# Cross attention on one core: a tile's probabilities turned in 32x32 blocks by VectorE and sent through DRAM, in place of sixteen TensorE transposes

## The chip, the core and the metric

The kernel runs on one core of a Trainium2 chip. The metric is the time of one execution on the device in microseconds (us). TensorE (PE) does the matmuls and the transposes, VectorE (DVE) and ScalarE (ACT) read the PSUM banks and do elementwise work, GpSimd (POOL) does elementwise work on SBUF, and SyncE (SP) issues every DMA, in program order. Each engine's order is the order in which the program is written.

## The reference

An encoder layer over 2 x 77 context rows, then a decoder layer over 2 x 2048 rows of width 512: causal self-attention, cross attention on the 77 encoded rows, and a feed-forward part of width 2048. All of it is float32. The part that matters here is the cross attention (16 heads of width 32, 77 keys):

```python
def _mha(xq, xkv, w_in, b_in, w_out, b_out, bias):
    ...
    scores = jnp.einsum('bhqd,bhkd->bhqk', q, k) / jnp.sqrt(jnp.asarray(hd, xq.dtype))
    scores = scores + bias[None]
    attn = jax.nn.softmax(scores, axis=-1)
    out = jnp.einsum('bhqk,bhkd->bhqd', attn, v)
    out = out.transpose(0, 2, 1, 3).reshape(Bq, Tq, D)
    return out @ w_out.T + b_out
...
y = y + _mha(yn, yn, dec_sa_in_w, dec_sa_in_b, dec_sa_out_w, dec_sa_out_b, sb)
y = y + _mha(_ln(y, dec_n2_s, dec_n2_b), memory, dec_ca_in_w, dec_ca_in_b, dec_ca_out_w, dec_ca_out_b, cb)
h = _ln(y, dec_n3_s, dec_n3_b)
y = y + (jax.nn.relu(h @ dec_ff1_w.T + dec_ff1_b) @ dec_ff2_w.T + dec_ff2_b)
```

## The kernel before

The 4096 decoder rows are eight blocks of 512 rows, each of four tiles of 128 rows. The first part of the program is the encoder and the self-attention, with the cross attention of block 0 (`first_cross`) strewn into it. The second part (TensorE's first product of it stands at 1632 us) is the feed-forward part of the eight blocks; the cross attention of block x+1 (`cross`) is laid between the products of block x.

The feed-forward part of a block has 56 slots (`ff_slot`). In slots 0 to 27 (`first_product`) a slot uses one weight tile of 256 KB; in slots 28 to 55 (`second_product`) four slots use 2, 2, 2 and 1 tiles, each with four matmuls of 128 columns (L1665). `feed` (L1539) reloads the ring `w_ring` of 16 such tiles at the end of each slot: it issues as many loads as tiles were used, each into the place of a tile that the slot has just finished, so SP waits for that slot's matmuls. In slots 28 to 31 `new_y` (L1359) also loads a 256 KB tile of the rows of the block after next, as long as there is one.

`cross` fills a table `plan` of 56 entries; before each `ff_slot` the stages of that slot's entry are written. A tile's attention (`attend_stages`) has the stages `score` (L822, then the bias, maxima and differences on VectorE), `exp` (ScalarE, L835), `sums` (VectorE, L840), `normalize` (GpSimd, L846), `turned`, and `times_v` (L860). `turned` makes 16 TensorE transposes of 128 x 77 into PSUM (L852) and four ScalarE copies to `pts` (L853), one buffer that the four tiles use in turn. Tile t has its stages at slots 13 + 5t plus 0, 2, 3, 3, 7 and 11. The products with the output weights (`o_product`, L1799) stand in slots 31 to 34 for tiles 0 and 1 and in 40 to 43 for tiles 2 and 3; the last normalization of the four tiles (`norm_stages`: statistics, centring, TensorE transposes L797) begins at slots 35, 36, 44 and 45.

PSUM has eight banks; in this part `bank()` hands out four in turn for the cross attention, and the feed-forward products hold the other four.

Of the kernel before, what the change touches and what calls it, by code (L numbers as in the profile page):

```python
# [10 lines left out]
F32 = mybir.dt.float32  # L11
AF = mybir.ActivationFunctionType
# [5 lines left out]
P = 128  # L18
B, T, S, D = 2, 2048, 77, 512
H, HD, DFF = 16, 32, 2048  # L20
# [3 lines left out]
MB = 512  # L24
# [30 lines left out]
def tile_encoder_decoder(ctx: ExitStack, tc: tile.TileContext, ins, out):  # L55
# [103 lines left out]
    with (  # L159
# [30 lines left out]
        def rows4(r):  # L190
            return slice(r * HD, (r + 1) * HD)
# [618 lines left out]
        def attend_stages(q, kTc, v, y, biased, pr, pts, place, w_o, bi=None):  # L810


            prh = pr.rearrange("p (h k) -> p h k", k=S)
            by_r = pr.rearrange("p (g r k) -> p g r k", r=HC, k=S)
            keep = {}

            def score():
                mx = sm.tile([P, NC, HC], F32, name="cmx", tag="cmx", bufs=3)
                banks = [bank() for _ in range(HC)]
                for g in range(NC):  # L820
                    for r in range(HC):
                        nc.tensor.matmul(  # L822
                            banks[r][:, ts(g, S)], q(g)[rows4(r)], kTc[rows4(r), g, :], start=True, stop=True
                        )
# [12 lines left out]
            def sums():  # L837
                su = sm.tile([P, H], F32, name="csu", tag="csu", bufs=2)
                ri = sm.tile([P, H], F32, name="cri", tag="cri", bufs=2)
                nc.vector.tensor_reduce(su, prh, AX.X, ALU.add)  # L840
                nc.vector.reciprocal(ri, su)
                keep["ri"] = ri

            def normalize():
                ri = keep["ri"]
                nc.gpsimd.tensor_tensor(prh, prh, ri[:, :, None].to_broadcast([P, H, S]), ALU.mult)  # L846

            def turned():
                for g in range(NC):
                    pt = bank()  # L850
                    for r in range(HC):
                        nc.tensor.transpose(pt[:S, ts(r, P)], prh[:, g * HC + r, :], ident)  # L852
                    nc.scalar.copy(pts(g), pt[:S, :])  # L853

            def times_v():
                ot = bank()
                for g in range(NC):
                    for r in range(HC):
                        h = g * HC + r
                        nc.tensor.matmul(  # L860
                            ot[rows4(r), ts(g, P)], v[:, ts(h, HD)], pts(g)[:, ts(r, P)], start=True, stop=True
                        )
                keep["oT"], keep["bank"] = place(), ot
                nc.scalar.copy(keep["oT"], ot)

            def out():
                mm, oT = bank(), keep["oT"]
                for c in range(NC):
                    nc.tensor.matmul(mm, oT[:, ts(c, P)], w_o[:, c, :], start=(c == 0), stop=(c == NC - 1))
                nc.vector.tensor_tensor(y(), mm, y(), ALU.add)  # L870

            return score, exp, sums, normalize, turned, times_v, out, keep

        def first_cross():
# [21 lines left out]
            def pts(g):  # L896
                return kT[:S, g, 2 * MB : 3 * MB]

            def loads():
                for t in range(TB):  # L900
# [667 lines left out]
        mixed = oflat[:, H * S : H * S + 12 * P].rearrange("p (k n) -> p k n", n=P)  # L1568
        lefts = {}

        def by_f(tile):
# [153 lines left out]
        def cross(x):  # L1725
# [79 lines left out]
            for n, js in Q_SLOTS.items():  # L1805
                plan[n].append(lambda js=js: [q_product(j) for j in js])
            for n, js in O_SLOTS.items():
                t = 0 if n < 36 else 2
                plan[n].append(lambda t=t, js=js: [o_product(t, j) for j in js])
            bias_1 = None  # L1810
            if m == 0:

                def next_batch():
                    nc.sync.dma_start(kTc, ckT_d[:, :, ts(b, S)])
                    nc.sync.dma_start(vc[0][:S, :], cv_d[:, b, :])

                plan[1].append(next_batch)

                spare = [y_of(x + 1, r) for r in range(HC)]
                bias_1 = [a[:, : NC * S].rearrange("p (g k) -> p g k", k=S) for a in spare]  # L1820
                plan[3].append(lambda: bias_tile(prs[0].rearrange("p (h k) -> p h k", k=S), 2, P, S, 255))
                plan[5].append(lambda: [bias_tile(a, 2, P, S, 255 - P, r, HC) for r, a in enumerate(bias_1)])
            for t in range(TB):
                at = 13 + 5 * t
                y = lambda t=t: y_of(x, t)
                biased = m == 0 and t < 2
                fs = attend_stages(
                    lambda g, t=t: qT[g // 2][:, g % 2, ts(t, P)], kTc, vc[0][:S, :], y, biased, prs[t % 2],
                    lambda g: pts_all[:S, g, :], place("xr"), wbt,
                    bias_1 if biased and t else None,  # L1830
                )
                held["o", t] = fs[7]
                if t % 2:
                    fs = fs[:5] + (lambda t=t, f=fs[5]: [f(), sums_o(t - 1)],)
# [4 lines left out]
                at = (35, 36, 44, 45)[t]  # L1839
                for k, f in zip((0, 2, 4), fs):  # L1840
                    plan[at + k].append(f)
                rows_later[x * per + 15 + t] = fs[3]
            for fs in plan:
                for f in fs:
# [84 lines left out]
        for n in range(end):  # L1929
# [21 lines left out]
            for step in script_of(n):  # L1951
                if step in ("a", "d"):
                    k = to_turn.pop(0)
                    turn([(n, k, r) for r in range(HC)], step)
                    turned.append(k)
                    assert len(turned) <= pts_all.shape[1]
                    leave(n, k)
                elif step == "E":
                    exps(1)
                elif step == "J":  # L1960
                    while parts:
                        parts.pop(0)()
                elif step == "j":
                    parts.pop(0)()
                elif step == "S" and may_score() and stream[0][0] <= n + 2:
                    two = stream[0][1] == 0 and may_score(1) and stream[1][0] == stream[0][0]
                    score_next(1 if two else 0)
                elif step in ("v", "V"):
                    values(n, turned, not to_turn, step == "V")
                    turned = []  # L1970
                elif step == "F":
                    feed(turned_to[n])
# [69 lines left out]
```

## Time and profile before

| | |
|---|---|
| median of 3 runs | 2705.1 us (2704.49 to 2707.9) |
| the profiled execution's own time | 2708.39 us |
| its span | 2706.3 us, mean granted TensorE clock 0.998 |
| TensorE, weight loads, VectorE, ScalarE, GpSimd busy | 99%, 81%, 68%, 56%, 37% |
| DMA | 385.10 MB, 142 GB/s over the span; 153 to 241 GB/s in the slices of the second part |

A profiled execution is about 3 us above the median. The rows of the trace name a line of the kernel, the engine, the operation, the tiles written and read, and the duration. TensorE's ends are modelled, so how long a group of matmuls holds it is read from where the next group starts.

### The profile page before, as it was taken

The numbers are of one execution on the slowest core, as the hardware profiler recorded it, in microseconds if no ns is written. First come the engines' busy times: TensorE is split into PE (matmuls) and PEld (weight loads), VectorE is DVE, ScalarE is ACT, GpSimd is POOL, SyncE is SP. The second block draws the span as 40 slices with busy tenths as digits, with TensorE's granted clock in tenths as the row PEclk, the third lists the DMA queues.
The fourth block names the chain that finished last, engine by engine and source line by source line (L and its number), as shares of the span: only waits on it lengthen the run. The fifth ranks groups of instructions, "written<-read, shape, count | busy, mean of one in ns | idle before, by whom it ended". The sixth has DMA issues, their size and how long they took to land.

```text
span 2706.3 us, 68257 instructions
## 1 busy us (share of the span) xinstructions
PE 2684.3 (99%) x26606; PEld 2199.2 (81%) x26606; DVE 1848.9 (68%) x5448; ACT 1526.2 (56%) x2960; POOL 1002.3 (37%) x844
## 2 busy tenths in 40 slices
PE   9999999999999999999999999999999999999998
PEld 6678777777776677778777887999999898989898
DVE  4776688888885687788888883737464746464635
ACT  3545567767886557777767794444443444444431
POOL 2602235500300513223300103556565555556546
PEclk9999999999999999999999999999999999999999
DMA  8734445511213522343311216565658565657575
GB/s 235 215 99 131 128 146 174 169 59 43 64 49 87 144 80 81 111 126 118 107 53 40 73 59 196 176 211 172 215 169 241 172 215 171 215 170 216 153 222 186
DMA packets 296276, 385.10 MB, mean 142 GB/s; under 512 B 41184, under 2 KB 165648, under 8 KB 295826
## 3 DMA queue, kind: packets, MB, share of 16 engines
q1 hardware_dynamic: 295954, 380.73, 46.9%
q8 instruction: 211, 3.46, 0.5%
q14 instruction: 111, 0.91, 0.1%
HBM read 334.15 MB, written 46.47 MB: 141 GB/s over the span
## 4 chain that ended last, share of the span: by engine, by line
PE 96%; DVE 1%; ACT 1%; DMA 1%; POOL 1%; SPq 0%; issue 0%; DVEq 0%; POOLq 0%; ACTq 0%
PE psum L417 18%; PE psum L1636 15%; PE psum L1665 13%; PE psum L375 11%; PE psum L441 9%; PE psum L1120 8%; PE psum L1799 3%; PE psum L1756 3%; PE psum L1035 3%; PE psum L852 2%; PE psum L822 1%; PE psum L860 1%; PE psum L576 1%; PE psum L797 1%; PE psum L239 1%; PE psum L215 1%
## 5 line engine op out<-in xcount | busy, mean ns | idle before, releaser
L406 ACT ACTIVATE pp<-pp,nm 128x128 f32<-128x128 f32 (+15 forms) x512 | 611.4, 1200 | 23.4 <-DVE nm L401 23.2
L384 DVE TENSOR_SCALAR_CACHE_REDUCE pp<-psum 128x512 f32<-128x512 f32 (+3 forms) x1024 | 556.7, 590 | 69.2 <-PE psum L375 67.1
L423 ACT COPY pts<-psum 128x512 f32<-128x512 f32 x696 | 374.4, 593 | 346.3 <-PE psum L417 309.5
L417 PE MATMUL psum<-ident,pp 128*128 128x128 f32 x4352 | 527.4, 276 | 5.7 <-ACT nT L310 4.0
L417 PEld LDWEIGHTS psum<-ident,pp 128*128 128x128 f32 x4352 | 475.2, 141 | 64.5 <-issue 21.4
L441 PEld LDWEIGHTS psum<-pts,vv 128*32 128x32 f32 x8704 | 225.7, 110 | 119.4 <-DVE pp L384 49.3
L375 PE MATMUL psum<-kT,q 32*128 32x512 f32 (+3 forms) x2560 | 320.3, 565 | 2.2 <-ACT kT L231 1.4
L421 DVE COPY pts<-psum 128x512 f32<-128x512 f32 x392 | 257.7, 686 | 84.8 <-PE psum L417 81.3
L1665 PE MATMUL psum<-pp 128*128 128x128 f32 x2560 | 304.5, 276 | 1.9 <-POOL pp L948 1.6
L1665 PEld LDWEIGHTS psum<-pp 128*128 128x128 f32 x2560 | 296.3, 192 | 8.6 <-issue 2.8
L441 PE MATMUL psum<-pts,vv 128*32 128x128 f32 x8704 | 278.0, 275 | 1.1 <-DVE pp L384 0.8
L948 POOL TENSOR_TENSOR pp<-pp 128x512 f32<-128x512 f32 x159 | 212.8, 1355 | 110.2 <-ACT pp L800 45.4
L1636 PE MATMUL psum<-vv,pp 128*128 128x256 f32 x1024 | 236.2, 381 | 0.0
L1636 PEld LDWEIGHTS psum<-vv,pp 128*128 128x128 f32 x1024 | 190.3, 190 | 25.8 <-issue 0.5
L391 DVE CUSTOM_DVE_ANT_0 pp<-psum,bias 128x256 f32<-128x256 f32 (+1 forms) x512 | 196.0, 411 | 13.2 <-PE psum L375 12.7
L375 PEld LDWEIGHTS psum<-kT,q 32*128 32x128 f32 x2560 | 127.5, 183 | 87.3 <-issue 50.0
L1649 DVE TENSOR_TENSOR kT<-kT,psum 128x512 f32<-128x512 f32 x96 | 65.8, 686 | 191.1 <-PE psum L1636 190.9
L1652 ACT ACTIVATE kT<-kT,vecs 128x256 f32<-128x256 f32 x192 | 86.9, 501 | 156.6 <-DVE kT L1649 155.9
L1636 PE MATMUL psum<-nT,pp 128*128 128x256 f32 x768 | 174.1, 380 | 0.0
L1636 PEld LDWEIGHTS psum<-nT,pp 128*128 128x128 f32 x768 | 144.2, 190 | 20.3 <-issue 1.6
L1673 ACT COPY oT<-psum 128x128 f32<-128x128 f32 x56 | 15.0, 268 | 239.1 <-PE psum L1665 239.1
L480 POOL TENSOR_TENSOR oT<-rirows,oT 128x512 f32<-128x512 f32 x30 | 38.4, 1279 | 288.6 <-DMA rirows<-rec 267.0
(272 smaller groups left out, 4108.2 us busy)
## 6 DMA issues: line engine op xcount, KB each, us to landing
pp<-w_d SPq DMA_DIRECT2D x520, 256.0 KB
pp<-in_dec_ff_wT_dram SPq DMA_DIRECT2D x112, 256.0 KB
bias<-tzg SPq DMA_DIRECT2D x128, 128.0 KB
pp<-wo_d SPq DMA_DIRECT2D x56, 256.0 KB
wqk<-in_dec_sa_in_wT_dram SPq DMA_DIRECT2D x52, 256.0 KB
wqk<-sa_q SPq DMA_DIRECT2D x84, 128.0 KB
vv<-in_enc_ff_wT_dram SPq DMA_DIRECT2D x8, 1024.0 KB
xr<-in_x_dram SPq DMA_DIRECT2D x32, 256.0 KB
```

Of the source, the lines that this page charges most:

```text
L375: nc.tensor.matmul(banks[r][:, : kn * P], q[rows4(r), ts(t, P)], kT[rows4(r), g, k0 * P : (k0 + kn) * P], start=True, stop=True,)
L384: nc.vector.tensor_scalar(p[:, k0 : k0 + far], s[:, :far], 1.0, None, ALU.mult, ALU.max, accum_out=st["mx"][:, r, c : c + 1],)
L391: nc.vector.tensor_tensor_reduce(p[:, k0 + far : i + 1], s[:, far:kn], near[:, 2 - (kn - far) :], 1.0, LOWEST, ALU.add, ALU.max, accum_out ...
L406: nc.scalar.activation(p, p, AF.Exp, bias=nm, accum_out=to)
L417: nc.tensor.transpose(pt[:, ts(x, P)], state[n]["p"][r][:, k], ident)
L421: nc.vector.tensor_copy(pts[:, : len(load), :], pt[:, :w])
L423: nc.scalar.copy(pts[:, : len(load), :], pt[:, :w])
L441: nc.tensor.matmul(ot[rows4(r)], vv[:, k, ts(g * HC + r, HD)], got.pop((n, k, r)), start=k == ks[0] and (whole or not begun), stop=k == ks ...
L948: engine.tensor_tensor(out, a, b, ALU.subtract)
L1120: nc.tensor.matmul(mm[:, ts(f, TOK)], left[:, c, ts(f, P)], right[:, c, :], start=c == 0, stop=c == 1,)
L1636: nc.tensor.matmul(mm[:, ts(f, TOK)], a[:, c, ts(f, P)], b[:, c, :], start=fresh and f == 0 and c == 0, stop=c == 1, skip_group_check=True,)
L1665: nc.tensor.matmul(psum[:, bank_i, ts(col, P)], lhs[:, c, :], w[:, c, :], start=fresh and k in (0, 3) and c == 0, stop=c == 3, skip_group_ ...
```

## The change

In `cross`, `turned` gives way to two stages. `turned_out` lets VectorE transpose the tile's probabilities in blocks of 32x32 (one instruction on 128 x 1536, so that the 77 keys of a head are padded to 96) into one buffer `stage`, and one DMA of 768 KB writes that to a DRAM tile `crossed` (two of them, in turn). `moved` brings it back with three DMAs of 256 KB, each for 32 keys, into the same `pts`; there a head's 128 queries now stand as four runs of 32. `times_v` reads them in that form. `first_cross` keeps the TensorE transposes.

The padding makes `prs` larger, and `stage` takes the last 1536 columns of the half of `pp` that held the ring: `w_ring` has 13 tiles in place of 16.

Each tile has its own slots, as tables: `TILES` (score, exp, sums, normalize, turned_out, moved, times_v), `OUTS` (the output products), `NORMS` (the last normalization).

```diff
+        def heads_of(pr):
+            return pr.rearrange("p (h k) -> p h k", h=H)[:, :, :S]
...
-                nc.scalar.activation(pr, pr, AF.Exp)
+                nc.scalar.activation(prh, prh, AF.Exp)
...
+            def turned_out():
+                pT = stage.rearrange("p (c h q) -> p c h q", h=H, q=RB)
+                nc.vector.transpose(pT, pr.rearrange("p (h c q) -> p c h q", h=H, q=RB))
+                nc.sync.dma_start(bounce.rearrange("c p x -> p c x"), stage.rearrange("p (c x) -> p c x", x=H * RB))
+
+            def moved():
+                for c in range(-(-S // RB)):
+                    nc.sync.dma_start(pts[ts(c, RB), :, :], bounce[c].rearrange("(a k) x -> k a x", k=RB))
...
+                        pT = pts[:S, g, ts(r, P)] if stage is None else pts[:S, :, ts(h, RB)]
                         nc.tensor.matmul(
-                            ot[rows4(r), ts(g, P)], v[:, ts(h, HD)], pts(g)[:, ts(r, P)], start=True, stop=True
+                            ot[rows4(r), ts(g, P)], v[:, ts(h, HD)], pT, start=True, stop=True
                         )
...
-        prs = [oflat[:, : H * S], pts_all[:, 5:8, :].rearrange("p a k -> p (a k)")[:, : H * S]]
+        PADDED = H * 3 * RB
+        prs = [oflat[:, :PADDED], pts_all[:, 5:8, :].rearrange("p a k -> p (a k)")]
+        stage = low[:, END // 2 - PADDED :]
+        crossed = [dram.tile([3, P, H * RB], F32, name=f"crossed{k}", tag=f"crossed{k}") for k in range(2)]
...
-        O_SLOTS = {at + k: js for at in (31, 40) for k, js in enumerate(((0, 1), (2, 3), (4, 5), (6,)))}
+        TILES = ((13, 16, 17, 17, 19, 23, 30), (18, 20, 20, 22, 25, 31, 32), (21, 25, 25, 28, 31, 33, 36), (27, 28, 33, 33, 36, 38, 43))
+        OUTS = ((33, 34, 36, 38), (44, 45, 46, 48))
+        NORMS = ((39, 42, 43), (42, 45, 49), (49, 50, 51), (49, 53, 54))
...
-        w_ring = [low[:, ts(j, D)] for j in range(16)]
+        w_ring = [low[:, ts(j, D)] for j in range((END // 2 - PADDED) // D)]
...
-                for k, f in zip((0, 2, 3, 3, 7, 11), fs):
-                    plan[at + k].append(f)
+                for k, f in zip(TILES[t], fs):
+                    plan[k].append(f)
```

How the tables move TensorE's work is seen at slots 28 to 34 of a block's feed-forward part. The line numbers of the changed file are higher: L1685 is L1665 of before, L873 is L860, L1819 is L1799, L1568 is L1548, L1376 is L1359. TensorE before, from slot 28 on:

```order
L1665 MATMUL psum<-pp,kT 128x128 x8
L860 MATMUL psum<-pts,q 32x128 x16
L1665 MATMUL psum<-pp 128x128 x8
L852 MATMUL psum<-ident,oT 77x128 x16
L1665 MATMUL psum<-pp 128x128 x8
L1799 MATMUL psum<-wbig,xr 128x256 x4
L1665 MATMUL psum<-pp,kT 128x128 x4
L1799 MATMUL psum<-pp,wqk 128x256 x4
```

The same slots in the changed kernel:

```order
L1685 MATMUL psum<-pp,kT 128x128 x8
L1685 MATMUL psum<-pp 128x128 x8
L873 MATMUL psum<-pts,q 32x128 x16
L1685 MATMUL psum<-pp 128x128 x8
L1685 MATMUL psum<-pp,kT 128x128 x4
L873 MATMUL psum<-pts,q 32x128 x16
L1685 MATMUL psum<-pp 128x128 x8
L1819 MATMUL psum<-wbig,xr 128x256 x4
```

The `times_v` of tile 0 and that of tile 1 are now apart by the twelve matmuls of slots 30 and 31, and no transposes stand there. SP's issues around the same place in the changed kernel (`crossed_244` and `crossed_245` are the two DRAM tiles, `y_0_3_80` the rows that `new_y` loads, from L861 and L865 on the two new stages):

```order
L861 DMA crossed_245<-pp 128x3x512
L1568 DMA pp<-w_d 128x512
L1568 DMA pp<-wo_d 128x512 x2
L1568 DMA pp<-w_d 128x512 x2
L1376 DMA vv<-y_0_3_80 128x512
L1568 DMA pp<-w_d 128x512
L1568 DMA pp<-wo_d 128x512
L1376 DMA vv<-y_0_3_80 128x512
L1568 DMA pp<-w_d 128x512 x2
L1376 DMA vv<-y_0_3_80 128x512
L865 DMA pts<-crossed_245 32x4x512 x3
L861 DMA crossed_244<-pp 128x3x512
```

Tile 1's `moved` (the row with x3) stands behind the two loads that `feed` issues at the end of slot 30 and behind that slot's `new_y`. Before, those rows read, without the two stages:

```order
L1548 DMA pp<-w_d 128x512 x3
L1359 DMA vv<-y_0_3_80 128x512
L1548 DMA pp<-w_d 128x512 x2
L1359 DMA vv<-y_0_3_80 128x512
L1548 DMA pp<-w_d 128x512 x2
L1359 DMA vv<-y_0_3_80 128x512
L1548 DMA pp<-w_d 128x512
```

All four tiles of all seven cross attentions in this part move in this way; SP's queue gains four DMAs for each.

More of the change, by code (lines that the diff above doesn't have):

```diff
@@ L808, in q_group, with attend_stages @@
             nc.vector.tensor_scalar(dst, mm, vec("dec_ca_in_b", o), SCALE, ALU.add, ALU.mult)
-        def attend_stages(q, kTc, v, y, biased, pr, pts, place, w_o, bi=None):
-            prh = pr.rearrange("p (h k) -> p h k", k=S)
-            by_r = pr.rearrange("p (g r k) -> p g r k", r=HC, k=S)
+        def heads_of(pr):
+            return pr.rearrange("p (h k) -> p h k", h=H)[:, :, :S]
+        def attend_stages(q, kTc, v, y, biased, pr, pts, place, w_o, bi=None, stage=None, bounce=None):
+            prh = heads_of(pr)
+            by_r = prh.rearrange("p (g r) k -> p g r k", r=HC)
             keep = {}
@@ L852, in turned @@
                         nc.tensor.transpose(pt[:S, ts(r, P)], prh[:, g * HC + r, :], ident)
-                    nc.scalar.copy(pts(g), pt[:S, :])
+                    nc.scalar.copy(pts[:S, g, :], pt[:S, :])
+            def turned_out():
[5 more added lines that the diff above has]
+                    nc.sync.dma_start(pts[ts(c, RB), :, :], bounce[c].rearrange("(a k) x -> k a x", k=RB))
             def times_v():
@@ L870, in out @@
                 nc.vector.tensor_tensor(y(), mm, y(), ALU.add)
+            if stage is not None:
+                return score, exp, sums, normalize, turned_out, moved, times_v, keep
             return score, exp, sums, normalize, turned, times_v, out, keep
@@ L894, in first_cross @@
             oT, xn = kT[:, 1, 3 * MB :], kT[:, 2, 3 * MB :]
-            def pts(g):
-                return kT[:S, g, 2 * MB : 3 * MB]
+            pts = kT[:, :, 2 * MB : 3 * MB]
             def loads():
@@ L1807, in cross @@
             for n, js in O_SLOTS.items():
-                t = 0 if n < 36 else 2
+                t = 0 if n in OUTS[0] else 2
                 plan[n].append(lambda t=t, js=js: [o_product(t, j) for j in js])
@@ L1820, in cross @@
                 bias_1 = [a[:, : NC * S].rearrange("p (g k) -> p g k", k=S) for a in spare]
-                plan[3].append(lambda: bias_tile(prs[0].rearrange("p (h k) -> p h k", k=S), 2, P, S, 255))
+                plan[3].append(lambda: bias_tile(heads_of(prs[0]), 2, P, S, 255))
                 plan[5].append(lambda: [bias_tile(a, 2, P, S, 255 - P, r, HC) for r, a in enumerate(bias_1)])
             for t in range(TB):
-                at = 13 + 5 * t
                 y = lambda t=t: y_of(x, t)
@@ L1828, in cross @@
                     lambda g, t=t: qT[g // 2][:, g % 2, ts(t, P)], kTc, vc[0][:S, :], y, biased, prs[t % 2],
-                    lambda g: pts_all[:S, g, :], place("xr"), wbt,
-                    bias_1 if biased and t else None,
+                    pts_all[:, :HC, :], place("xr"), wbt, bias_1 if biased and t else None, stage, crossed[t % 2],
                 )
@@ L1833, in cross @@
                 if t % 2:
-                    fs = fs[:5] + (lambda t=t, f=fs[5]: [f(), sums_o(t - 1)],)
-                for k, f in zip((0, 2, 3, 3, 7, 11), fs):
-                    plan[at + k].append(f)
+                    fs = fs[:6] + (lambda t=t, f=fs[6]: [f(), sums_o(t - 1)],)
+                for k, f in zip(TILES[t], fs):
+                    plan[k].append(f)
                 fs = norm_stages(y, "n3", bo, place("xt"), lambda t=t: nTt[:, :, ts(t, P)])
-                at = (35, 36, 44, 45)[t]
-                for k, f in zip((0, 2, 4), fs):
-                    plan[at + k].append(f)
+                for k, f in zip(NORMS[t], fs):
+                    plan[k].append(f)
                 rows_later[x * per + 15 + t] = fs[3]
```

5 lines of the change are left out of this document (3 added, 2 removed).

## The prediction

> **What bounds the kernel now.** I read the page first: engines, slices and the chain that ended last; then TensorE's waits and the chain at one cross attention, and last the queue of SP and the DMA load at the place to which the tables move the work.
>
> ```profile
> PE 2684.3 (99%) x26606; PEld 2199.2 (81%) x26606; DVE 1848.9 (68%) x5448; ACT 1526.2 (56%) x2960; POOL 1002.3 (37%) x844
> PE   9999999999999999999999999999999999999998
> PE 96%; DVE 1%; ACT 1%; DMA 1%; POOL 1%; SPq 0%; issue 0%; DVEq 0%; POOLq 0%; ACTq 0%
> ```
>
> TensorE is busy in every slice, and 96% of the chain is its own work. So every microsecond taken out of its stream is a microsecond of the span, and every wait put into it is one too. Its waits in the whole run, longest first and further down:
>
> ```profile
> PE psum L417 <- ACT nT L310: 4.0, 2, 2.2
> ...
> PE psum L1665 <- POOL pp L948: 1.6, 2, 1.2
> ```
>
> None of its waits is ended by a DMA: the loads come early enough everywhere. That is what the change puts at risk.
>
> **What is taken away.** The chain at one tile's transposes, score and `times_v`:
>
> ```profile
> 1697.75 1.75 PE psum L852 x16
> ...
> 1704.68 1.06 PE psum L822 x32
> ...
> 1707.67 1.01 PE psum L860 x32
> ...
> 1710.60 1.75 PE psum L852 x16
> ```
>
> A tile's 16 transposes hold TensorE for 1.75 us. They go from 7 cross attentions of 4 tiles: 28 x 1.75 = 49.0 us. The ScalarE copies go with them:
>
> ```profile
> L853 ACT COPY pts<-psum x112: 564/584/603, 1698.3 to 2564.9; 77x512 f32<-77x512 f32 x112
> ...
>   PEld psum L852: 1.1, 7
> ```
>
> That is 112 x 0.584 = 65 us off an engine that is not on the path, worth nothing, and 1.1 us in which the transposes waited for banks. Gain: 50.1 us, or 50.1 / 7 = 7.2 us a block. **This 7.2 us is the measure for all that follows.**
>
> **What VectorE gets.** One transpose of 128 x 1536 a tile, in no row of this size. The nearest:
>
> ```profile
> L470 DVE STREAM_TRANSPOSE rt<-ri x30: 211/211/214, 55.8 to 1507.8; 128x32 f32<-128x32 f32 x30
> L840 DVE TENSOR_REDUCE csu<-oT x14: 1435/1436/1437, 1689.6 to 2537.6; 128x16 f32<-128x1232 f32 x14
> 1700.00:1800.00 100.00, 100.00 (x850) 92.18 (x849) 61.37 (x122) 40.88 (x89) 60.67 (x54) 1.00 0.69 211
> ```
>
> If 0.211 us were paid for each 32 columns it would be 48 x 0.211 = 10.1 us; at L840's pace per element 1536 / 1232 x 1.44 = 1.8 us. I take 1.8, since 0.211 us for 32 columns is mostly a fixed part. VectorE is busy 61 of 100 us there and has room for 4 x 1.8 a block: nothing on the path. At 10.1 it would be nearly full, and its reads of PSUM would hold TensorE. `exp` and `bias_tile` on the padded form touch as many elements as before: nothing. `times_v` now reads four runs of 32 columns; no row has such an operand. I take no difference (at worst its 1.01 us doubles).
>
> **The return, on the path.** In slots 28 to 31 TensorE has seven weight tiles of the second products and tile 0's `times_v`; then it needs tile 1's `pts`. The group of 56 records is seven tiles, up to the start of the next group:
>
> ```profile
> 1879.34 6.42 PE L1665 MATMUL psum<-pp 128*128 128x128 f32 x56
> 1885.59 0.60 PE L797 MATMUL psum<-ident,xt 128*128 128x128 f32 x4
> ```
>
> 6.25 us for seven, 0.89 a tile; so from the start of slot 28 TensorE is at tile 1's `times_v` after 6.25 + 1.01 = 7.3 us. Slot 31 is one tile, so it is there 0.89 us after the matmuls of slot 30. SP can issue tile 1's three loads only behind the reload of slot 30, which waits for those matmuls, and behind a row load. How SP follows a slot's end today (slot 28: TensorE passes on at 1994.49):
>
> ```profile
> 1992.51 2.05 PE L1665 MATMUL psum<-pp,kT 128*128 128x128 f32 x16
> 1994.49 1.08 PE L860 MATMUL psum<-pts,q 77*32 77x128 f32 x32
> ...
> 1991.55 3.36 SPq L1548 DMA_DIRECT2D pp<-w_d  x3
> 1994.96 0.42 SPq L1359 DMA_DIRECT2D vv<-y  x1
> ```
>
> The reload's issue ends at 1994.91 and the row load's at 1995.38, 0.9 us after the matmuls. Three more issues of 0.42 end 2.2 us after. When the queue is quiet a small return through DRAM looks like this:
>
> ```profile
> 1542.60 1.82 SPq L478 DMA_DIRECT2D rirows<-rec  x4
> ...
> 1546.13 1.29 POOL L480 TENSOR_TENSOR oT<-rirows,oT 128x512 f32<-128x512 f32 x1 [3.94 <-DMA rirows<-rec]
> ```
>
> From the end of the last issue (1544.42) to the use 1.7 us. So the loads are there 3.9 us after slot 30, and TensorE waits 3.9 - 0.9 = 3.0 us. That is the lower bound. But the queue is not quiet. The same slots before (the last two columns are the DMA engines' busy share and GB/s):
>
> ```profile
> 1994.50:1999.50 5.00, 5.00 (x67) 4.64 (x67) 4.90 (x12) 2.28 (x5) 2.35 (x3) 1.00 0.79 216
> 1999.50:2004.50 5.00, 5.00 (x36) 4.72 (x35) 2.96 (x5) 1.75 (x3) 3.46 (x3) 1.00 0.86 242
> ```
>
> 216 / 0.79 and 242 / 0.86 give some 277 GB/s for full engines: 0.95 us for 256 KB. From slot 28 on SP issues six weight tiles, three row loads and the three loads of the return, twelve of 256 KB. The first is issued 0.9 + 0.3 us in and lands some 1.7 + 0.7 later (the rows of the quiet return are 64 KB each, and 192 KB more take 0.7), at 3.6; eleven more at 0.95 end at 14.0. TensorE was there at 7.3: a wait of 6.8 us, the upper bound. The loaded windows are of this very place, so I take 6.5. The last cross attention has no row loads beside it: nine transfers, 3.6 + 8 x 0.95 = 11.2, a wait of 3.9 at most and 2.5 at least; 3.5 taken. Sum: 6 x 6.5 + 3.5 = **42.5 us**.
>
> The other returns are covered: tile 0 has six slots between `moved` and `times_v`. Tile 2 has slots 33 to 35, five weight tiles (4.5 us), and three groups of output products:
>
> ```profile
> 2001.08 1.89 PE L1799 MATMUL psum<-wbig,xr 128*128 128x256 f32 x8
> 2002.80 1.05 PE L1665 MATMUL psum<-pp,kT 128*128 128x128 f32 x8
> ```
>
> At 1.7 us each that is 9.6 us against the 3 to 7 of a return; tile 3 has four slots and more. While SP waits for VectorE's transpose or for the write to DRAM, the reloads behind it wait too; the ring's 13 tiles (11.6 us of work at 0.89; 14.3 before) cover that, so nothing. Without that cover each microsecond of delay would be paid.
>
> **The clock.** A TensorE that idles costs more than the idle time. The two longest gaps, and the windows around them (the granted clock is the third column from the end):
>
> ```profile
> 108.19 1.10 PE L417 MATMUL psum<-ident,pp 128*128 128x128 f32 x8 [1.83 <-ACT nT L310]
> 114.17 2.82 PE L417 MATMUL psum<-ident,pp 128*128 128x128 f32 x12 [2.20 <-ACT nT L310]
> ...
> 104.00:108.00 4.00, 2.35 (x28) 1.09 (x24) 3.96 (x19) 3.76 (x12) 3.38 (x3) 1.00 0.24 85
> 112.00:116.00 4.00, 1.83 (x9) 1.83 (x10) 1.24 (x6) 2.59 (x8) 3.49 (x3) 0.74 0.82 240
> 116.00:120.00 4.00, 4.00 (x19) 3.60 (x18) 1.07 (x4) 2.97 (x11) 3.92 (x5) 0.83 0.14 51
> ```
>
> After 1.83 us the clock stays at 1.00; after 2.20 it is at 0.74 and 0.83 for two windows, 4 x 0.26 + 4 x 0.17 = 1.7 us of lost clock. A wait of 3 to 7 us should do the same once a block. Some of the slow stretch may fall into the wait itself: between 0 and 1.7 a block, 1.5 taken, 7 x 1.5 = **10.5 us**. [...]
>
> **The end of a block.** Tile 2's statistics, centring and transposes now follow in slots 49, 50 and 51 (44, 46 and 48 before). The steps before:
>
> ```profile
> 2039.05 0.68 DVE L779 BATCH_NORM_STATS2 bnst<-vv 128x6 f32<-128x512 f32 x1
> ...
> 2041.54 0.27 POOL L783 TENSOR_SCALAR crs<-cmv,crs 128x1 f32<-128x1 f32 x1
> ...
> 2041.84 0.82 ACT L789 ACTIVATE xt<-vv,crs 128x512 f32<-128x512 f32 x1 [0.84 <-POOL crs L783]
> ```
>
> 3.6 us from 2039.05 to 2042.66, against two slots of four tiles, 3.6 us: between no wait and 1 us, 0.4 taken, **3 us** for seven.
>
> **The sum:** -50.1 + 42.5 + 10.5 + 3 = +5.9 us. The profiled execution took 2708.4 us itself (span 2706.3) and would take 2714.3; on the median of 2705.1 that is 2711. A change within 0.2% (5.4 us) could hardly be told from none; the forecast lies just beyond it.
>
> **The rivals.**
> *A quick return* (the other side): the three loads get through as if the queue were quiet, 7 x 3.0 = 21 us, and the sum is -50.1 + 21 + 10.5 + 3 = -15.6, 2690; without loss of clock 2679. For it: 14 to 21% of the DMA engines' time is free in the two windows. Against it: nine loads stand ahead. It decides below 7.2 us a block for wait and clock together. [...]
> *The clock holds*: 5.9 - 10.5 = -4.6, 2700. For it only that one gap of 1.83 went unpunished.
> *The DMA engines become the bound in slots 28 to 55.* There 61 transfers of 256 KB (49 weight tiles, 8 for the output products, 4 row loads) become 76 with the 15 of the bounce: 76 x 0.95 = 72 us. TensorE has 49 x 0.89, eight groups of output products (six at 1.7, two half as long: 12), 4 for `times_v` and 2 for the last transposes: 62, with wait and clock 70. If the ring of 13 doesn't hide the difference, 2.5 us a block are added: 2711 + 15 = 2726.
> *VectorE's transpose takes 10 us*: its evictions come late, 3 us a block or more, 2732.
>
> **How the numbers follow.** The forecast (waits of 5.5 to 7.5 us, 2700 to 2722) 0.45, of which 0.28 is slower by over 0.2%, 0.15 the same and 0.02 faster; the quick return 0.22, faster; the clock that holds 0.13, of which 0.08 the same and 0.05 faster; the DMA bound 0.15 and the slow transpose 0.05, slower. Faster 0.29, same 0.23, slower 0.48. The range leaves out half of the quick return and the slow transpose: 2685 to 2728.
>
> **What would show it.** Right: no L852 rows in the second part; before the second L873 of a block a TensorE gap of some 6.5 us ended by the DMA `pts<-crossed`, seven in all, the last shorter; PEclk below 1.00 behind each; a STREAM_TRANSPOSE near 1.8 us. Wrong: gaps near 3 us, or none; a clock at 1.00 throughout; TensorE waiting for weight tiles or for VectorE. If the gaps are under 5 us the sign turns.

## The result and the profile after

The changed kernel takes 2746.1 us (median of 4 runs, 2743.74 to 2747.19) against 2705.1 before: ratio 1.0148, 95% interval 1.0131 to 1.0166. The forecast was 2711 with a range of 2685 to 2728; slower was right, the size was not. The profiled execution took 2745.24 us, its span 2743.5, its mean granted clock 0.983.

From the page of the changed kernel: busy time, TensorE's slices, the chain that ended last. Then the longest of TensorE's waits (us in total, times, longest), which has no counterpart before.

```profile
PE 2659.3 (97%) x26158; PEld 2174.0 (79%) x26158; DVE 1902.2 (69%) x5476; ACT 1471.9 (54%) x2848; POOL 993.9 (36%) x844
PE   9999999999999999999999999898989898989998
PE 90%; DMA 5%; DVE 2%; SPq 1%; ACT 1%; POOL 1%; issue 1%; DVEq 0%; POOLq 0%; ACTq 0%
```

```profile
PE psum L873 <- DMA pts<-crossed: 64.3, 12, 8.8
```

The 8s among TensorE's slices are the waits for the return. Seven of the twelve are tile 1's (8.32, 8.12, 8.64, 7.55, 8.78, 8.40 and, in the last cross attention, 6.17: 56.0 us), five are tile 3's (8.3 us together). TensorE around the third of them, then SP's queue at that place:

```profile
2001.74 1.08 PE L873 MATMUL psum<-pts,q 77*32 77x128 f32 x32
2002.75 2.05 PE L1685 MATMUL psum<-pp 128*128 128x128 f32 x16
2004.63 1.06 PE L1685 MATMUL psum<-pp,kT 128*128 128x128 f32 x8
2014.33 1.94 PE L873 MATMUL psum<-pts,q 77*32 77x128 f32 x32 [8.64 <-DMA pts<-crossed]
2016.20 3.78 PE L1685 MATMUL psum<-pp 128*128 128x128 f32 x16
2019.77 2.52 PE L1819 MATMUL psum<-wbig,xr 128*128 128x256 f32 x8
2022.13 1.95 PE L1685 MATMUL psum<-pp 128*128 128x128 f32 x16
```

```profile
2003.94 1.21 SPq L1568 DMA_DIRECT2D pp<-w_d  x2
2005.20 0.42 SPq L1376 DMA_DIRECT2D vv<-y  x1
2005.68 1.37 SPq L865 DMA_DIRECT2D pts<-crossed  x3
```

Slot 30's matmuls end at 2004.63; SP has issued the three loads by 2007.05, 2.4 us later; TensorE starts on them at 2014.33. The rows behind the wait show a second loss: sixteen matmuls take 3.78 us at 2016.20 and 1.95 at 2022.13. The clock explains it. Windows of half clock behind three waits (PE busy is the second figure; the last three columns are granted clock, DMA share and GB/s):

```profile
1761.70:1765.00 3.30, 3.30 (x10) 2.70 (x10) 2.44 (x7) 0.57 (x1) 2.38 (x3) 0.50 0.78 277
1867.50:1877.60 10.10, 4.81 (x46) 4.46 (x47) 2.70 (x6) 0.59 (x1) 3.40 (x4) 0.50 0.69 223
2010.90:2021.00 10.10, 6.67 (x51) 6.10 (x52) 2.86 (x5) 0.59 (x1) 2.04 (x3) 0.50 0.57 190
```

TensorE worked 6.67 us at half clock behind the wait that ended at 2014.33, so 3.3 us are lost there; over the nine such stretches 26.0 us (busy time at clock 0.50, halved; "lost clock" below is always this). Before, the second part had none.

The account of the spans: -50.1 (transposes) + 64.3 + 26.0 = +40.2, against 2743.5 - 2706.3 = +37.2. The second part began 2.7 us earlier than before (at 1629.7 us, not 1632.4), which closes the account; over the profiled executions of all kernels it begins at 1627.0 to 1633.2, so this is scatter of the first part.

### The profile page after: what moved, and what is told of

Same layout as the page of the kernel before. It is cut to its first block, busy times and chain, and to the rows that moved or that the text cites. A ratio compares the mean times of both kernels' runs of the same rounds, so it can differ in the third digit from the quotient of the medians.

```text
span 2743.5 us, 67349 instructions
## 1 busy us (share of the span) xinstructions
PE 2659.3 (97%) x26158; PEld 2174.0 (79%) x26158; DVE 1902.2 (69%) x5476; ACT 1471.9 (54%) x2848; POOL 993.9 (36%) x844
## 4 chain that ended last, share of the span: by engine, by line
PE 90%; DMA 5%; DVE 2%; SPq 1%; ACT 1%; POOL 1%; issue 1%; DVEq 0%; POOLq 0%; ACTq 0%
PE psum L417 18%; PE psum L1656 14%; PE psum L1685 11%; PE psum L375 10%; PE psum L441 9%; PE psum L1134 8%; DMA pts<-crossed 3%; PE psum L1819 3%; PE psum L1776 3%; PE psum L1049 3%; PE psum L873 1%; PE psum L825 1%; PE psum L576 1%; PE psum L239 1%; PE psum L797 1%; PE psum L215 1%
## 5 line engine op out<-in xcount | busy, mean ns | idle before, releaser
L1685 PE MATMUL psum<-pp 128*128 128x128 f32 x2560 | 318.7, 283 | 1.8 <-POOL pp L962 1.6
L1685 PEld LDWEIGHTS psum<-pp 128*128 128x128 f32 x2560 | 309.2, 198 | 12.0 <-issue 6.1
```

What stands on the lines that cost most here:

```text
L1685: nc.tensor.matmul(psum[:, bank_i, ts(col, P)], lhs[:, c, :], w[:, c, :], start=fresh and k in (0, 3) and c == 0, stop=c == 3, skip_group_ ...
```

## The experiments

In the table "waits" are TensorE's waits over 0.25 us in the second part, except the 1.9 us at its end that every kernel has; waits and lost clock, less 50.1, give the difference of the span to the 2706.3 of before to within some 5 us (with the fill its own work comes on top). Spans and waits are those of the profiled execution, which can lie off the median.

| kernel | median us | ratio to before, interval | waits us | lost clock us | profiled span us |
|---|---|---|---|---|---|
| changed | 2746.1 | 1.0148, 1.0131 to 1.0166 | 64.3 | 26.0 | 2743.5 |
| fill | 2730.4 | 1.0090, 1.0073 to 1.0106 | 20.3 | 9.8 | 2736.1 |
| loads earlier | 2739.3 | 1.0114, 1.0099 to 1.0129 | 55.4 | 23.6 | 2731.0 |
| rows later | 2736.7 | 1.0106, 1.0091 to 1.0121 | 52.7 | 27.3 | 2736.1 |
| spread tables | 2708.5 | 1.0002, 0.9993 to 1.0012 | 33.9 | 20.3 | 2709.3 |
| no write and no loads | 2668.6 | 0.9856, 0.9841 to 0.9871 | 8.7 | 0 | 2664.2 |
| one load, 96 partitions | 2741.5 | 1.0127, 1.0105 to 1.0150 | 66.8 | 19.9 | 2738.7 |
| one load, spread tables, rows later | 2693.2 | 0.9947, 0.9932 to 0.9961 | 26.1 | 6.8 | 2688.0 |
| three loads, spread tables, rows later | 2688.5 | 0.9931, 0.9917 to 0.9946 | 23.3 | 10.2 | 2688.3 |
| runs of 8 KB in DRAM | 2775.8 | 1.0257, 1.0241 to 1.0273 | 86.0 | 38.1 | 2780.8 |
| sums of tile 3 at 34 | 2696.4 | 0.9958, 0.9945 to 0.9971 | 22.6 | 6.8 | 2689.8 |
| no write | 2741.0 | 1.0129, 1.0112 to 1.0146 | 62.7 | 20.6 | 2736.1 |
| weights as source | 2747.8 | 1.0152, 1.0134 to 1.0169 | 68.7 | 24.3 | 2746.0 |
| sums of tile 3 at 33 | 2674.1 | 0.9883, 0.9868 to 0.9898 | 13.4 | 0 | 2671.8 |
| loads on 128 partitions | 2723.6 | 1.0075, 1.0058 to 1.0092 | 48.2 | 20.4 | 2719.5 |

### Is all of the loss the return?

The write and the three loads are left out:

```diff
-                nc.sync.dma_start(bounce.rearrange("c p x -> p c x"), stage.rearrange("p (c x) -> p c x", x=H * RB))
...
-                for c in range(-(-S // RB)):
-                    nc.sync.dma_start(pts[ts(c, RB), :, :], bounce[c].rearrange("(a k) x -> k a x", k=RB))
+                pass
```

> The changed kernel with its tables and VectorE's transpose, but without the write to DRAM and without the three loads back: times_v works on whatever stands in pts, so part of the computation is left out. Theory (all of the loss is the return: 64.3 us of waits and 26 us of lost clock; tables, ring of 13 and VectorE's transpose cost nothing): 2705 - 50 = 2655, to 2660; no TensorE wait over 1 us in the second part, clock 1.00. Rival (the tables or the smaller ring cost something themselves, hidden behind the waits so far): 2670 or more, with waits for banks or for weight tiles.

2668.6 us, 38.5 below the before of the same chip, mean granted clock 0.998 as before. So the transposes were worth what the prediction took for them, and VectorE's transposes, the ring of 13 and the padding cost at most a few us. One wait is new, which the 8 us for the return had hidden:

```profile
PE psum L1817 <- DVE vv L1821: 8.7, 7, 2.2
```

It is the output products of slot 34 (L1817 in this file, L1819 in the changed kernel) that wait for VectorE's adds: the tables themselves cost 8.7 us, so the rival had a part of the truth.

### Is the half clock the price of idling?

64 transposes of the identity, which nobody reads, are put ahead of tile 1's `times_v`, where TensorE waits anyway:

```diff
+                if t == 1:
+                    fs = fs[:6] + (lambda f=fs[6]: [warm(64), f()],)
```

> The changed kernel with 64 transposes of the identity ahead of tile 1's times_v in each block (7.0 us of TensorE work at 0.109 us each, into an unused bank), so that TensorE works while the loads come. Theory (TensorE's wait for tile 1's return costs twice: 6.2 to 8.8 us of idling, and then a halved clock, 26 us in all in the changed kernel, nearly all behind tile 1): the clock stays at 1.00 behind tile 1, the remaining wait there is 0 to 1.8 us, the fill costs nothing where the wait was longer than 7 us, and the time falls by some 20 to 24 us, to about 2724. Rival (the clock falls because of times_v's small matmuls and not because of the idle time): the clock stays low in the same places and the time is that of the changed kernel, 2746.

2730.4, 15.7 below the changed kernel on the medians. The profiled execution was the slowest of the four (2737.9), and its span is 7.4 us shorter than the changed kernel's. Waits that remain:

```profile
PE psum L873 <- DMA pts<-crossed: 20.3, 11, 3.7
```

Lost clock went from 26.0 to 9.8 us; 6.4 of the 9.8 stand behind tile 3's waits, which nothing fills, and only 3.4 behind tile 1's, where it was 20.8. The fill does not bring the data sooner: what was wait is now wait and fill, seven times 7.1 us and 20.3, some 70 us in place of 64.3. So most of the clock's loss can be had back with work that is worth nothing, and the half clock hangs on the idling and not on `times_v`. The expectation of 2724 was missed by about the clock that is still lost.

### What stands ahead of the return

Tile 1's `moved` one slot earlier; in another kernel the rows of the block after next at slots 42 to 45, not 28 to 31:

```diff
-        TILES = (..., (18, 20, 20, 22, 25, 31, 32), ...)
+        TILES = (..., (18, 20, 20, 22, 25, 30, 32), ...)
```

> The changed kernel with tile 1's moved at slot 30 instead of 31: SP issues the three loads right after tile 0's times_v, ahead of slot 30's two weight tiles and its row load, and TensorE has slot 30's 1.8 us more work before it needs them. Theory (the loads are late because of what stands ahead of them on the loaded DMA engines): the wait falls by 1.8 us of work and by about three transfers of 0.8 us, from 8.0 to about 4 us, so by 28 us over seven, with some more if the clock recovers sooner: 2712 to 2720. Rival (the return through DRAM itself is slow, whatever stands ahead): the wait falls by the 1.8 us alone, 2733.

```diff
-            if FIRST <= n < FIRST + TB:
-                new_y(x + 2, n - FIRST)
+            if FIRST + 14 <= n < FIRST + 14 + TB:
+                new_y(x + 2, n - FIRST - 14)
```

> The changed kernel with the four row loads of a block (new_y) at slots 42 to 45 instead of 28 to 31, so that three transfers of 256 KB fewer stand ahead of tile 1's return. Theory (load on the DMA engines): the wait in the first six blocks falls from 8.3 to that of the last block, about 6.2, which has no row loads: 13 us less, 2733. Rival (row loads do not matter, the last block's wait is short for another reason): 2746.

The earlier loads were a miss: 2739.3, tile 1's waits 45.9 in place of 56.0, 1.4 us a block. I had counted both the 1.8 us of TensorE work by which the loads are issued sooner and the three transfers that no longer stand ahead. At the block shown above SP was indeed done with them 2.6 us sooner, counted from the start of slot 28. But from the last issue to TensorE's start it then took 7.8 us on average over the seven blocks, not 6.6. Why is not shown; full engines are not the whole reason, since shortly before the last issue ended (at 2001.74 in this kernel) they were mostly free (share 0.28):

```profile
2000.50:2001.50 1.00, 1.00 (x12) 1.00 (x11) 1.00 (x3) 1.00 (x2) 0.03 (x1) 1.00 0.28 88
```

The rows behaved as expected: the six waits that have row loads beside them fell from 8.3 to 6.2 on average, the seventh, which has none, stayed (6.17 and 6.33).

The write ahead of it is not what tile 1 waits for. Here it is done for the first two tiles only:

```diff
+                if wrote[0] < 2:
                     nc.sync.dma_start(bounce.rearrange("c p x -> p c x"), stage.rearrange("p (c x) -> p c x", x=H * RB))
+                wrote[0] += 1
```

> The changed kernel, but the write of the turned probabilities to DRAM is done for the first two tiles alone; all loads stay and bring back old data, so part of the computation is left out. Theory (the transfers of 768 KB that were issued a few slots ahead leave the engines behind, so the queue is not empty when the reloads of slot 28 begin): tile 1's waits fall from 8.0 to about 6.5, tile 3's vanish, 2746 - 21 = 2725. Rival (the write has landed by then and only the loads' own slow packets and the twelve transfers count): waits fall by less than 0.7 us, 2738 or more.

2741.0: the rival. Tile 3's waits went, tile 1's did not (62.7 us for seven, 9.0 each, where the changed kernel has 8.0; why it is more is not known). It also speaks against transfers left over from ahead of slot 28 as what tile 1's return waits for. In the five us around the start of that slot the engines are at a share of 0.50 here (second row) and of 0.95 in the changed kernel (first row), and the waits that follow are alike, 8.66 and 8.64 us:

```profile
1996.07:2001.07 5.00, 5.00 (x46) 4.71 (x40) 4.90 (x9) 2.36 (x6) 2.27 (x1) 1.00 0.95 286
1992.28:1997.28 5.00, 5.00 (x46) 4.71 (x40) 4.90 (x8) 2.36 (x6) 2.27 (x1) 1.00 0.50 143
```

### The pace of the return itself

Tile 2's return has little beside it. A window inside it, and one with weight tiles alone, both of the changed kernel:

```profile
2022.70:2026.70 4.00, 4.00 (x31) 3.79 (x30) 3.70 (x8) 0.27 (x1) 2.24 (x1) 1.00 1.04 245
2037.00:2040.00 3.00, 3.00 (x29) 3.00 (x29) 2.53 (x8) 0.00 (x0) 2.90 (x4) 1.00 1.07 402
```

In both the engines are full (share 1.04 and 1.07), yet one moves 245 and the other 402 GB/s: a 2 KB packet takes some 140 ns in the first (median) and 84 in the second. Four kernels vary one side of the load each; in the first two the layout in DRAM and with it the write change too. One load onto 96 partitions, key 32c+k on partition 3k+c, rows of `v` in the same order:

```diff
-                nc.sync.dma_start(bounce.rearrange("c p x -> p c x"), stage.rearrange("p (c x) -> p c x", x=H * RB))
+                nc.sync.dma_start(bounce, stage)
...
-                for c in range(-(-S // RB)):
-                    nc.sync.dma_start(pts[ts(c, RB), :, :], bounce[c].rearrange("(a k) x -> k a x", k=RB))
+                nc.sync.dma_start(pts[: 3 * RB, :, :], bounce.rearrange("(a k) (c x) -> (k c) a x", k=RB, c=3))
```

> The changed kernel with the three loads of 32 partitions replaced by one load of 96: key 32c+k now stands on partition 3k+c, the rows of v in the same order, zeros for the 19 padded ones. Bytes and tables as they were. Theory (a 2 KB packet that goes to a destination of only 32 partitions is slow, 140 ns against 84 in the trace of the changed kernel, so the engines move the return at some 225 GB/s where they move weight tiles at over 340; and two issues of 0.45 us fall away): 1.4 us of data time (about 0.9 if 96 partitions aren't quite as quick as 128) and 0.9 us of issues less, so tile 1's waits go from 8.0 to about 6.0, tile 3's nearly vanish: 7 x 2 + 4 = 18 us, 2728. Rival (the packets are slow because of how the DRAM side is read, in 2 KB pieces of four places, whatever the destination): only the issues are saved, waits about 7.2, 2740.

Runs of 8 KB in DRAM, the write in four:

```diff
+                for a in range(HC):
+                    nc.sync.dma_start(bounce[:, :, a, :].rearrange("c k x -> k c x"), stage[ts(a, RB)].rearrange("p (c x) -> p c x", c=3))
...
+                    nc.sync.dma_start(pts[ts(c, RB), :, :], bounce[c])
```

> The changed kernel's tables and its three loads on 32 partitions each, but the DRAM tile is laid out so that a load reads 8 KB in one run for each partition (before: four runs of 2 KB, 64 KB apart); the write now goes in four DMAs of 32 partitions in place of one. Theory (the loads' packets are slow because of the pieces on the DRAM side): during the return the engines move over 300 GB/s in place of 225, tile 1's waits fall by 3 x 0.4 = 1.2 us to about 6.8, 2746 - 12 = 2734. Rival (the destination, few partitions with four packets each, sets it): 225 GB/s again, waits of 8 us and 2746, or a little more by the three additional issues of a write.

Weight tiles as the source:

```diff
+                    nc.sync.dma_start(pts[ts(c, RB), :, :], w2_d[0, c].rearrange("(a k) x -> k a x", k=RB))
```

> The changed kernel, but the three loads of a return read three weight tiles in DRAM (in the same row order, onto the same 32 partitions) in place of the turned probabilities, which are still written; part of the computation is left out. The return then has nothing to wait for but SP and the DMA engines. Theory (the place on the chip to which a load goes sets its pace, whatever it reads): its packets take some 145 ns per 2 KB again, tile 1's waits stay at 7.5 to 9 us, 2740 to 2750. Rival (the DRAM tile that is read, just written and 768 KB in one piece, is what is slow, or the wait is for the write): packets at 84 ns, waits of 6.5 us or less, 2730 or less.

All 128 partitions as the destination:

```diff
+                    nc.sync.dma_start(pts[:, c, :], bounce[c])
```

> The changed kernel, but each of the three loads of a return puts its 256 KB onto all 128 partitions (128 x 512, as a weight tile is loaded) and not onto 32; the probabilities then stand in the wrong places, so part of the computation is left out. Bytes, issues and order are the same. [...] Rival (pts as a place, or loads behind other loads, and not the partitions): some 250 GB/s again, 2740 or more.

The same place, tile 2's return, in these four (96 partitions, 8 KB runs, weights, 128 partitions; clock, share and GB/s at the end of each row):

```profile
2022.50:2026.50 4.00, 4.00 (x31) 3.79 (x30) 3.71 (x7) 0.00 (x0) 3.11 (x2) 1.00 1.07 251
```

```profile
2035.00:2039.00 4.00, 4.00 (x31) 3.79 (x30) 3.37 (x7) 0.00 (x0) 3.48 (x2) 1.00 0.96 197
```

```profile
2026.80:2030.80 4.00, 4.00 (x32) 3.82 (x31) 3.11 (x6) 0.00 (x0) 3.77 (x2) 1.00 1.05 250
```

```profile
2012.80:2014.80 2.00, 2.00 (x15) 1.84 (x14) 1.97 (x5) 0.23 (x1) 0.79 (x1) 1.00 0.95 341
```

What is read makes no difference (250); longer runs don't help (197), nor does one load over 96 partitions (251). All 128 partitions bring 341. That 8 KB go to each partition is not the reason either: before, one load of 1 MB puts 8 KB onto each of 128 partitions, and its packets of 8 KB take 309 ns (median), where those of the 8 KB runs onto 32 partitions take 594. The window of that load:

```profile
1546.00:1549.00 3.00, 3.00 (x52) 2.80 (x42) 3.00 (x11) 3.00 (x7) 1.29 (x1) 1.00 0.91 353
```

And the pace shows in the waits of the kernel with 128 partitions:

```profile
PE psum L873 <- DMA pts<-crossed: 48.2, 7, 7.5
```

Tile 3's waits are gone and tile 1's fell by 1.1 us each; with 5.6 us less of lost clock the kernel took 2723.6, 22.6 us below the changed one (2727 was expected if the partitions set the pace). So the narrow destination is the price of 16 us of waits: in the windows above weight tiles on 128 partitions went 402 / 245 = 1.6 times as fast as the return onto 32. Why one load onto 96 gains nothing over 32 (251 against 245) is not shown.

The kernel with the 8 KB runs lost 30 us more: fourteen waits for the return. Its four writes read 32 partitions each, which may be slow for the same reason; that was not tried apart.

```profile
PE psum L874 <- DMA pts<-crossed: 86.0, 14, 12.9
```

### Tables that give the return its time

Tile 0's `times_v` at slot 27 in place of 30 (its return then has four slots), tile 1's return at 27 (five slots), and tile 3's sums, normalization, `turned_out` and `moved` one or two slots earlier:

```diff
-        TILES = ((13, 16, 17, 17, 19, 23, 30), (18, 20, 20, 22, 25, 31, 32), (21, 25, 25, 28, 31, 33, 36), (27, 28, 33, 33, 36, 38, 43))
+        TILES = ((13, 16, 17, 17, 19, 23, 27), (18, 20, 20, 22, 25, 27, 32), (21, 25, 25, 28, 31, 33, 36), (27, 28, 31, 31, 35, 37, 43))
```

> The changed kernel with other slots: tile 0's times_v at 27, tile 1's moved at 27 (SP issues it ahead of slot 27's reload, and TensorE has 9 us of work before tile 1's times_v at 32), tile 3's sums and normalize at 31, turned_out at 35, moved at 37. Theory (the loss is the two returns that are not covered, tile 1's and tile 3's, and the clock behind them): no wait for pts, clock 1.00, and the 50 us of transposes come out in full: 2655 to 2662. Rival (the 44 MB more make the DMA engines the bound of the second products, so that covering these two waits only makes others): weight tiles or other returns late, TensorE waits of 20 us and more, 2675 or above.

2708.5, the same as before, 50 us short of the theory. The return's waits fell from 64.3 to 18.9 us (the first and last of these rows), but a new one came and the clock went on losing 20.3:

```profile
PE psum L873 <- DMA pts<-crossed: 15.5, 10, 2.8
PE psum L825 <- ACT xr L877: 12.4, 7, 2.4
...
PE psum L873 <- issue: 3.4, 2, 2.8
```

At slot 27 tile 3's `score` (L825) needs four PSUM banks, one of which tile 0's `times_v` has filled just ahead of it and ScalarE has not copied out. The next kernels put tile 3's `score` at 28 and the rows at slots 46 to 49, with one load and with three:

```diff
-..., (27, 28, 31, 31, 35, 37, 43))
+..., (28, 30, 31, 31, 35, 37, 43))
```

> The load on 96 partitions, and tables that spread the stages: times_v of tile 0 at slot 27 and tile 1's return at 27 instead of 30 and 31, score of tile 3 at 28 (behind, not beside, the copy out of tile 0's bank), rows of the block after next at slots 46 to 49. Theory (what is left in the spread tables of before, 34 us of waits and 20 of clock, is one bank conflict of 12.4 us, returns that are 1 to 3 us late, and half clocks behind these): waits under 10 us in all and clock under 6, so 2705 - 50 + 15 = 2670. Rival (a return takes what it takes, and the DMA engines are the bound): waits for pts of 15 us and more again, or waits for weight tiles in their place, 2690 or more.

> The same tables and rows at slots 46 to 49, but with the three loads of 32 partitions as in the changed kernel. Theory (both halves matter): the bank conflict's 12.4 us go, the returns stay 1 to 3 us late for one or two tiles a block, 2685 to 2695. Rival (the form of the load hardly matters once there are enough slots): within 5 us of the kernel with both.

2693.2 and 2688.5: both below before, by 0.5% and 0.7%, and the one load is no gain here either. The waits of the second one:

```profile
PE psum L1819 <- DVE vv L1823: 17.2, 7, 2.8
PE psum L873 <- DMA pts<-crossed: 4.1, 3, 2.1
```

The return is nearly paid; the wait has moved to VectorE, which comes to the adds of slot 33 late. Its queue there:

```profile
1986.12 1.76 DVE L860 STREAM_TRANSPOSE pp<-oT 128x1536 f32<-128x1536 f32 x1
1987.82 1.39 DVE L843 TENSOR_REDUCE csu<-pts 128x16 f32<-128x1232 f32 x1
...
1991.46 2.66 DVE L962 TENSOR_TENSOR pp<-pp,kT 128x512 f32<-128x512 f32 x2
1994.04 0.94 DVE L1823 TENSOR_TENSOR vv<-vv,psum 128x256 f32<-128x256 f32 x2
```

Tile 2's transpose and tile 3's sums (L843) stand in one slot ahead of the adds (L1823). The sums, with the normalization, move to slot 34, and `turned_out` and `moved` one slot later; or to 33, behind the output products, with the rest as it was:

```diff
-..., (28, 30, 31, 31, 35, 37, 43))
+..., (28, 30, 34, 34, 36, 38, 43))
```

> The spread tables with the rows at slots 46 to 49, and sums and normalization of tile 3 at slot 34 in place of 31, its turned_out at 36 and moved at 38. Theory (the 17 us in which the output products of slot 33 wait for VectorE come from the 1.8 us transpose of tile 2 and the 1.6 us of tile 3's sums standing together ahead of the adds): 14 of these 17 us and half of the 10 us of lost clock go, 2688 - 19 = 2670; the kernel without the bounce took 2668. Rival (VectorE is behind by the scores at slot 28, or tile 3's return is now late): waits of 15 us and more, for VectorE or for pts, 2682 or more.

```diff
-..., (28, 30, 31, 31, 35, 37, 43))
+..., (28, 30, 33, 33, 35, 37, 43))
```

> The spread tables with rows at 46 to 49 and tile 3's sums and normalization at slot 33, behind the output products of that slot on VectorE, in place of 31; turned_out and moved of tile 3 stay at 35 and 37. Theory (the waits for VectorE come from tile 3's sums ahead of the adds, the waits for pts with sums at 34 from turned_out and moved one slot later): 10 of the 17 us for VectorE go and no waits for pts come, 2677 to 2682. Rival (one stage shifted late always shows up in the next): 2688 to 2697 as in the two kernels beside it.

At 34 the waits for VectorE fell to 7.2 us, but those for the return rose to 15.0, and the time to 2696.4 (2686.56 to 2704.38 over nine runs): the rival. At 33 both are small:

```profile
PE psum L1819 <- DVE vv L1823: 7.0, 7, 1.1
PE psum L873 <- DMA pts<-crossed: 4.8, 5, 2.1
```

No clock is lost, and the kernel takes 2674.1 us: 32.6 below the before of the same chip, and the best of all that compute the whole result. It is within 6 us of the one without any bounce.

## Why the prediction was off

Between the forecast of 2711 and the 2746.1 lie 35 us. Four terms of the sum make 34 of them: the clock 15.5, tile 1's return 13.5, tile 3's return 8.3, and the norm chain 3 the other way.

- *The gain, -50.1:* right. The kernel without the bounce came out at -38.5 on the medians and -42.1 on the spans, where -50.1 + 8.7 of new waits is -41.4.
- *VectorE's transpose at 1.8 us:* right. Of the 0.211 us for 32 columns an estimated 0.18 are a fixed part, by a straight line through them and the 1.766 us for 1536.

```profile
L860 DVE STREAM_TRANSPOSE pp<-oT x14: 1764/1766/1769, 1695.1 to 2578.5; 128x1536 f32<-128x1536 f32 x14
```

- *The ScalarE copies worth nothing, the weight tiles covered by a ring of 13:* right; no TensorE wait for a weight tile was seen, though the DMA engines went from a share of 0.64 (second row) to 0.74 in the second part. That rival fell (seven times its 2.5 us would be 17.5, not 15; nothing hangs on it), and with it the slow transpose.

```profile
1640.00:2740.00 1100.00, 1031.90 (x7716) 930.83 (x7714) 632.75 (x1140) 369.88 (x793) 579.81 (x498) 0.96 0.74 226
```

```profile
1640.00:2700.00 1060.00, 1058.11 (x8171) 957.28 (x8170) 580.34 (x1114) 425.67 (x908) 588.81 (x499) 1.00 0.64 194
```

- *The wait for tile 1's return, 42.5 us:* the place and the mechanism were right (seven gaps ahead of the second `times_v` of a block, the last shorter), the size was not: 56.0. SP's part was right, 2.4 us to the end of the last issue against 2.2 taken. The step that failed is "eleven more at 0.95": it priced the three loads of the return as weight tiles. With 128 partitions as the destination the waits were 48.2 us, so 7.8 of the 13.5 us are the narrow destination. The other 5.7 (0.8 a wait) are not settled. The kernel without the write speaks against transfers left over from ahead of slot 28. Nor are the engines full all the way, as the step took them to be: in the 3 us behind the last issue they moved 227 GB/s at a share of 0.75:

```profile
2007.00:2010.00 3.00, 0.00 (x0) 0.00 (x0) 2.02 (x4) 0.00 (x0) 3.00 (x4) 1.00 0.75 227
```

  The upper bound, added up in the same way, was no bound.
- *"The other returns are covered":* wrong for tile 3, 8.3 us in five waits: in these TensorE started 6.6 to 8.8 us after the last issue, where the prediction took 3 to 7 for a return. The waits were gone with 128 partitions, and also without the write: on a quicker or a less loaded path its five slots do.
- *The clock, 10.5 us:* mis-sized, 26.0 measured. The step that failed took the two dim windows behind a gap of 2.20 us as the price of any gap. Behind a wait of 6 to 9 us the half clock lasted 10.24 us, of which 4.2 to 7.1 fell into the work that followed: 2.1 to 3.6 us lost where 1.5 was taken, 20.8 in all. Two of tile 3's waits, which the sum did not have, cost another 5.1.
- *The norm chain, 3 us:* no such wait is in the trace; 0.
- *The sum:* -50.1 + 64.3 + 26.0 against -50.1 + 42.5 + 10.5 + 3. The quick return at 3.0 us a block was far off: 8.0 were measured.

## What to carry to other kernels

Where data go through DRAM to be turned, count from the last issue to the landing at the pace of the actual destination: here a load onto 32 partitions held the engines at 245 GB/s, where weight tiles on 128 went at 402. Give such a return more slots than that, and then look for what was hidden under the old wait: here it was a PSUM bank and then VectorE's queue. Price an idle TensorE at its wait plus what the clock takes afterwards, 26.0 us on 64.3 here.

## What the runs showed of the hardware that was not expected

- *The half clock comes late and stays.* In the changed kernel it lasted 10.24 us behind each of tile 1's seven waits of 6.17 to 8.78 us: it began 2.8 to 5.2 us after TensorE fell idle and ended 4.2 to 7.1 us after the work had begun again. Behind tile 3's wait of 3.55 us (second row) it lasted 6.83 us, behind that of 2.45 us 3.41, from 1.8 us after the work had begun again; tile 3's other waits, up to 1.12 us, had none.

```profile
1724.10:1734.30 10.20, 7.13 (x52) 6.44 (x53) 2.86 (x5) 0.59 (x1) 2.24 (x3) 0.50 0.62 197
2471.70:2478.40 6.70, 6.70 (x48) 5.69 (x40) 2.64 (x7) 1.30 (x2) 3.31 (x4) 0.50 0.67 211
```

  The kernel with tile 3's sums at 34, whose longest wait in the second part was 2.2 us, lost 6.8 us of clock; the best kernel, with waits up to 2.1 us, lost none:

```profile
1640.00:2665.00 1025.00, 1009.80 (x7705) 909.05 (x7704) 631.49 (x1136) 370.88 (x793) 587.24 (x498) 1.00 0.79 243
```

  The prediction's two gaps were 1.83 us without and 2.20 with. How long a wait must be for the half clock to follow is not shown.
- *A load's pace differed with the partitions that it reached:* 245 GB/s onto 32, 251 onto 96, 341 to 402 onto 128, with the engines at a share of 0.91 to 1.07. That 96 is no better than 32 is not explained.
